# Last block of a decoder: expert tiles' results stored by ScalarE, and dense pairs' exponentials issued two segments behind their scores

## The chip, the cores and the metric

The kernel runs on one core of a Trainium2 chip. The metric is the time of one execution on the device in microseconds (us). The core has five engines with an instruction queue each: TensorE (PE; its weight loads are shown as PEld), VectorE (DVE), ScalarE (ACT), GpSimd (POOL) and SyncE (SP). SyncE computes nothing; it issues DMA transfers. Other engines can issue transfers too, and an engine that issues one spends time of its own queue on it. An engine works through its queue in order; semaphores make it wait for the others.

## The reference

The program is a decoder of six sub-blocks on `x` of 16 samples x 256 positions x 256 features, f32, each with a LayerNorm ahead and a residual add behind. The change lies in the last one, in which each of 8 heads picks one of 8 experts for its values and one for its output:

```
q = (x @ w_q) -> 8 heads of 64;   k = (x @ w_k) -> 8 heads of 64
gates = sigmoid(x @ w_gate)                     # position, head, expert
gm = one_hot(argmax(gates)) * gates             # one expert per position and head
values = einsum('bhne,ehdk,bnd->bhnk', gm, value_experts, x)
attn = softmax(causal(q / 8 @ k.T))
out = attn @ values
out = einsum('bhne,ehkd,bhnk->bhnd', gm, output_experts, out)
x = x + out.sum(heads)
```

## The kernel before, in words

**Two ways through the output experts.** A *pair* is two heads of one sample; there are 4 pairs a sample. The first 13 samples (52 pairs) go the *sparse* way, the last 3 samples (12 pairs) the *dense* way.

In the sparse way the attention outputs of a pair, already scaled by gate and softmax sum, are scattered by GpSimd's indirect DMAs (L1673) into DRAM arrays `zd`, one for each head, in which the rows stand sorted by expert. Then 136 *units* work on these rows. A unit is 2 tiles of 128 rows of one head. `load2` (L1709) has SyncE load it from `zd` into one of six buffers, up to six units ahead of its use; `transposed2` transposes both tiles on TensorE into a PSUM buffer `ps_z2` (L1718) and ScalarE copies that to `zT` (L1720); `expert5` multiplies each tile by its expert's weights on TensorE into `po_t` (L1736), ScalarE copies the result to `y` (L1741, three buffers in turn), and a 256 KB transfer takes `y` to a DRAM array `yd` (L1742). Units of two neighbouring heads alternate, and up to two later units are transposed ahead of a unit's products. When all 34 units of a pair of heads are through, GpSimd gathers rows of `yd` back to the samples' order by indirect DMA (L1685), and VectorE adds them to `x` (L1692).

In the dense way a pair's outputs go through all eight output experts: the gates are broadcast to 64 partitions by two 512 KB loads on SyncE (L1836, `w<-gd`), VectorE multiplies the attention output by each, and 32 products on TensorE add up in one PSUM buffer `po` (L1865) over the four pairs of a sample.

**The order of the work** is written out by hand: inside this block the program keeps the order of the code on TensorE, VectorE, GpSimd and ScalarE. A loop over steps `s` does one sparse pair at a time in a pipeline of stages (`step5`), with `spot5` between the stages: a spot puts in at most one unit, further additions, and gathers that can start. From step 52 on, each step also starts a dense pair (`pair5`, a generator). A `yield` ends a *segment* of a pair. At each step, `advance` runs one segment of each live pair, ordered by a key that the pair itself gave: 0 attention products and the multiplications by the gates (of the pair started four steps ago), 1 scores (one step ago), 2 transposes of the second head (three steps ago), 3 queries and keys (this step), 5 output products (five steps ago), 6 preparations for a later sample, 9 scaling by the softmax sums, gate loads, gated values and transposes of the first head (two steps ago). After each segment `between` runs; from step 52 on it puts in two spots.

**The scores segment** (`causal_pair`, L244 to L264): TensorE writes the scores of the pair into `sc`, of which there is one buffer (L244); VectorE adds the causal mask (L249) and takes the row maxima (L259); the exponentials (L264, one for each half of the rows and each head, four in all) are ScalarE's. For dense pairs they are handed back as a function and put into the list `deferred`, which is worked off when all segments of the step are through, so behind the transposes' copies (`head_T`, L290) of the segment with key 9. The next user of `sc` is the next step's scores segment.

All other products of the block share one PSUM pool `mm` of four buffers, taken in turn: `ps_qk` (queries and keys, copied by ScalarE, L1510 and L1511), `ps_ve` (gated values, read by VectorE, L1525), the heads' transposes `tr` (L289; copied to `pT` by ScalarE, L290), `av`, `ps_z2` and `po_t`.

Of the 136 stores of units, 68 are issued from 3057 to 3297 us of the profiled span, 34 from 3321 to 3455 and 34 from 3549 to 3652; the dense steps start at about 3510.

Of the kernel before, what the change touches and what calls it, by code (L numbers as in the profile page):

```python
# [27 lines left out]
def decoder(ctx: ExitStack, tc: tile.TileContext, a: dict, out: bass.AP):  # L28
# [3 lines left out]
    nc = tc.nc  # L32
# [1420 lines left out]
    with ExitStack() as st:  # L1453
# [36 lines left out]
        def mm5(shape, name):  # L1490
            return psum.tile(shape, F32, tag="mm", name=name, bufs=4)
# [4 lines left out]
        def takes(us):  # L1496
            clock["pe"] += us
# [4 lines left out]
        def queries_keys(b, hp):  # L1502
            takes(1.7)
            hT = hTs5[b]
            cols = slice(hp * P, (hp + 1) * P)
            ps = mm5([P, 2, S], "ps_qk")
            for i in range(2):
                two_k(ps[:, i, :], lambda c: wfqk[i][:, c, cols], lambda c: hT[:, c, :])
            qk = pool.tile([P, 2, S], F32, tag="qk", name="qk", bufs=2)
            nc.scalar.mul(qk[:, 0, :], ps[:, 0, :], 0.125)  # L1510
            nc.scalar.copy(qk[:, 1, :], ps[:, 1, :])  # L1511
            return qk

        def gated_values(b, hp, vv, t):

            takes(3.4)
            tv = pool.tile([P, 2, 8, 64], F32, tag="tv", name="tv", bufs=1)
            for j in range(2):
                ps = mm5([P, 8, 64], "ps_ve")
                two_k(  # L1520
                    ps.rearrange("p e k -> p (e k)"),
                    lambda c: hTs5[b][:, c, t * P : (t + 1) * P],
                    lambda c: wve[hp][:, j, c, :],
                )
                nc.vector.tensor_tensor(  # L1525
                    tv[:, j], ps,
                    gms5[b][:, t, 2 * hp + j, :].unsqueeze(2).to_broadcast([P, 8, 64]), ALU.mult,
                )
            nc.vector.tensor_tensor(tv[:, :, 0:4, :], tv[:, :, 0:4, :], tv[:, :, 4:8, :], ALU.add)
            nc.vector.tensor_tensor(tv[:, :, 0:2, :], tv[:, :, 0:2, :], tv[:, :, 2:4, :], ALU.add)  # L1530
            nc.vector.tensor_tensor(vv[:, t], tv[:, :, 0, :], tv[:, :, 1, :], ALU.add)
# [199 lines left out]
        def expert5(u, at):  # L1731
            q, j, g = UNITS[u]
            zT = zT2s.pop(u)
            po = mm5([P, 2, D], "po_t")
            for i in range(2):
                nc.tensor.matmul(  # L1736
                    po[:, i, :], lhsT=zT[:, i, :],
                    rhs=w_oe[:, bass.ds(at[i] + 2048 * q, D)], start=True, stop=True,
                )
            y = pool.tile([P, 2, D], F32, tag="y5", name="y5", bufs=3)  # L1740
            nc.scalar.copy(y, po)  # L1741
            nc.sync.dma_start(  # L1742
                out=yds[2 * q + j][2 * P * g : 2 * P * (g + 1), :]
                .rearrange("(i p) d -> p i d", p=P),
                in_=y,
            )
# [73 lines left out]
        def pair5(b, hp):  # L1820
            gm = gms5[b]
            n = 4 * b + hp
            qk = queries_keys(b, hp)
            yield 1
            takes(0.9)
            (pr, sm), exps = causal_pair(pool, psum, qk, bufs=1, keep=2, small=4)
            deferred.append(exps)
            yield 9
            nc.vector.reciprocal(sm, sm)
            for qt, sl, w in ((0, slice(0, P), P), (1, slice(P, 384), S)):  # L1830
                for j in range(2):
                    nc.scalar.mul(pr[:, j, sl], pr[:, j, sl], sm[:, qt, j : j + 1])
            gr = grs[n % 2]
            for j in range(2):
                h = 2 * hp + j
                nc.sync.dma_start(  # L1836
                    out=gr[64 * j : 64 * j + 64].rearrange("p e s -> p (e s)"),
                    in_=gds5[b][8 * h : 8 * h + 8, :]
                    .rearrange("e s -> (e s)")
                    .partition_broadcast(64),  # L1840
                )
            vv = pool.tile([P, 2, 2, 64], F32, tag="vv", name="vv", bufs=2)
            for t in range(2):
                gated_values(b, hp, vv, t)
                spot5(step_at[0])
            pT = pool.tile([P, 2, 384], F32, tag="pT", name="pT", bufs=2)
            for j in range(2):
                head_T(pr, pT, j)
                yield 2 if j == 0 else 0
            takes(0.9)  # L1850
            av = mm5([P, S], "av")
            causal_pair_av(av, lambda t, j: vv[:, t, j, :], pT)
            ut = uts[(n + 1) % 2]
            for g in range(2):
                es = slice(4 * g, 4 * g + 4)
                nc.vector.tensor_tensor(
                    ut[:, es, :], gr[:, es, :], av.unsqueeze(1).to_broadcast([P, 4, S]), ALU.mult
                )
            yield 5
            if hp == 0:  # L1860
                pos[b] = psum.tile([P, 2, 512], F32, tag="po", name="po", bufs=1)
            po = pos[b][:, :, 0:D]
            for t in range(2):
                for e in range(8):
                    nc.tensor.matmul(  # L1865
                        po[:, t, :], lhsT=ut[:, e, t * P : (t + 1) * P], rhs=woe[hp][:, e, :],
                        start=(hp == 0 and e == 0), stop=(hp == 3 and e == 7),
                    )
                takes(3.5)
                if t == 0:  # L1870
                    spot5(step_at[0])
            if hp == 3:
                nc.vector.tensor_tensor(xs[b], xs[b], po, ALU.add)  # L1873
                nc.sync.dma_start(out=out[b].rearrange("(t p) d -> p t d", p=P), in_=xs[b])
# [26 lines left out]
        deferred = []  # L1901
# [5 lines left out]
        def new_before(b):  # L1907
            return (6, before5(b, mm5))

        with tc.manual_schedule(engines={mybir.EngineType.PE, mybir.EngineType.Pool, mybir.EngineType.DVE,  # L1910
                                         mybir.EngineType.Activation}):
            s = 0
            while s < END or live or gath or gathering:
                more = []
                step_at[0] = s
                if s < NSB:
                    def gates(b=s):
                        ohs5[b] = gates5(b, mm5, gms5[b], gval[:, 2 * b : 2 * b + 2, :]
                                         .rearrange("p t h -> p (t h)"))
                    more.append(gates)  # L1920
                if 0 <= s - 1 < NSB:
                    more.append(lambda: ranks5(s - 1))
                if s + 2 < NSB and s >= 0:
                    more.append(lambda: rows5(s + 2, mm5, h5[0]))
                for b, q in scat.get(s + 1, ()):
                    if q == 0:
                        back5(b)
                sc = list(scat.get(s, ()))
                for b, q in sc:
                    scatter5(b, q, 0, False)  # L1930

                def second(sc=sc):
                    for b, q in sc:
                        scatter5(b, q, 1, True)
                loads5(s)
                if s < NS + 3:
                    more.append(second)
                    step5(s, more)
                else:
                    second()  # L1940
                if s + 3 < NSB:
                    h5 = [normed(5, s + 3)]
                if s >= NSB:
                    next(plan, None)
                if s == NS - 4:
                    advance(live, [new_before(NSB)])
                elif live or NS <= s < END:
                    new = []
                    if NS <= s < END:
                        b, q = DENSE[s - NS]  # L1950
                        new.append((3, pair5(b, q)))
                        if q == 2 and b + 1 < NB:
                            new.append(new_before(b + 1))

                    def between():
                        if s >= NS:
                            spot5(s)
                            spot5(s)

                    advance(live, new, between)  # L1960
                    while deferred:
                        deferred.pop(0)()
                if s >= END:
                    for _ in range(4):
                        takes(2.0)
                        spot5(s)
                s += 1
# [74 lines left out]
```

## Time and profile before

| | |
|---|---|
| median of 3 runs | 3822.43 us (3819.25 to 3825.97) |
| profiled execution | 3819.31 us; its span 3817.5 us |
| mean granted clock of TensorE | 0.98 |
| TensorE busy | 3588.7 us (94%) |
| VectorE busy | 2290.7 us (60%) |
| ScalarE busy | 1732.0 us (45%) |
| GpSimd busy | 1352.8 us (35%) |
| last block with units, 3100 to 3660 us: TensorE idle | 20.7 + 28.5 + 25.1 us |
| the rest, 3660 to 3817 us: TensorE idle | 11.8 us |

The profile is of one execution; its span runs from the first instruction to the last, and the time of the execution has 1.8 us more. The idle rows come from the busy time by stretch (3100 to 3300, 3300 to 3510, 3510 to 3660, 3660 to 3817). In the groups and timelines, `L244` is line 244 of the kernel, `out<-in` are the program's names for what an instruction writes and reads, and a bracket such as `[2.44 <-ACT pr L264]` gives the engine's idle time just before the instruction and what ended it. `ACTq` and `SPq` are the queues of transfers that ScalarE and SyncE issue.

### The profile page before, as it was taken

The numbers are of one execution on the slowest core, as the hardware profiler recorded it, in microseconds if no ns is written. First come the engines' busy times: TensorE is split into PE (matmuls) and PEld (weight loads), VectorE is DVE, ScalarE is ACT, GpSimd is POOL, SyncE is SP. The second block draws the span as 40 slices with busy tenths as digits, with TensorE's granted clock in tenths as the row PEclk, the third lists the DMA queues.
The fourth block names the chain that finished last, engine by engine and source line by source line (L and its number), as shares of the span: only waits on it lengthen the run. The fifth ranks groups of instructions, "written<-read, shape, count | busy, mean of one in ns | idle before, by whom it ended". The sixth has DMA issues, their size and how long they took to land. (4 is left out here: it accounts for less than half of the span.)

```text
span 3817.5 us, 66392 instructions
## 1 busy us (share of the span) xinstructions
PE 3588.7 (94%) x23024; PEld 2585.0 (68%) x23024; DVE 2290.7 (60%) x6518; ACT 1732.0 (45%) x5178; POOL 1352.8 (35%) x1764
## 2 busy tenths in 40 slices
PE   8999999999999999969999889999999998888899
PEld 6777776777777777759987666665655565555566
DVE  6666667655555565542226776777897643546465
ACT  4555554555555555524435555665322243332431
POOL 3333332233433343342224553222005523545441
PEclk9999999999999999979999999999999999999999
DMA  8000000010000000032234100000000033343553
GB/s 291 1 1 1 1 1 1 1 59 10 17 18 15 12 18 15 15 89 73 71 111 166 29 23 19 29 29 7 8 18 29 25 117 118 110 128 86 165 154 88
DMA packets 190823, 207.16 MB, mean 54 GB/s; under 512 B 56944, under 2 KB 159800, under 8 KB 188960
## 3 DMA queue, kind: packets, MB, share of 16 engines
q1 hardware_dynamic: 160288, 142.68, 12.2%
q0 software_dynamic: 25168, 51.85, 4.8%
q10 hardware_dynamic: 5040, 8.40, 0.7%
q8 instruction: 189, 3.10, 0.4%
q14 instruction: 138, 1.13, 0.1%
HBM read 122.93 MB, written 79.92 MB: 53 GB/s over the span
## 5 line engine op out<-in xcount | busy, mean ns | idle before, releaser
L289 PEld LDWEIGHTS tr<-ident,pr 128*128 128x128 f32 x2176 | 276.3, 142 | 160.7 <-issue 89.7
L201 PE MATMUL ps_ve<-w_ve,w 128*128 128x512 f32 x768 | 364.8, 619 | 11.2 <-DVE tv L1525 3.3
L289 PE MATMUL tr<-ident,pr 128*128 128x128 f32 x2176 | 346.4, 275 | 25.4 <-ACT zT L528 10.4
L483 POOL TENSOR_TENSOR pr<-pr,sm 128x512 f32<-128x512 f32 x256 | 264.4, 1055 | 282.3 <-DVE sm L481 142.0
L279 POOL TENSOR_TENSOR pr<-pr,sm 128x256 f32<-128x256 f32 (+1 forms) x256 | 206.5, 828 | 424.0 <-DVE sm L277 313.4
L477 ACT ACTIVATE pr<-sc,nmx 128x256 f32<-128x256 f32 x512 | 237.1, 472 | 251.1 <-DVE nmx L472 174.0
L1673 POOL DMA_INDIRECT zd<-zu,slots x208 | 208.0, 1000 | 395.8 <-DVE slots L1595 187.1
L273 ACT ACTIVATE pr<-sc,nmx 128x128 f32<-128x128 f32 (+1 forms) x512 | 209.8, 418 | 266.8 <-DVE nmx L271 225.7
L1685 POOL DMA_INDIRECT g<-yo,slots x208 | 205.2, 987 | 267.8 <-DVE x L1692 188.9
L472 DVE CUSTOM_DVE_ANT_0 sc<-sc,mk 128x256 f32<-128x256 f32 x512 | 211.2, 444 | 112.1 <-PE sc L462 59.4
L1525 DVE TENSOR_TENSOR tv<-ps_ve,gms 128x512 f32<-128x512 f32 x208 | 140.6, 688 | 216.0 <-PE ps_ve L201 161.7
L201 PE MATMUL ps_qk<-hT,w_a 128*128 128x256 f32 x1024 | 258.8, 386 | 0.0
L201 PEld LDWEIGHTS ps_ve<-w_ve,w 128*128 128x128 f32 x768 | 145.2, 199 | 165.7 <-issue 141.2
L290 DVE COPY pT<-tr 128x384 f32<-128x384 f32 (+1 forms) x384 | 223.2, 594 | 18.9 <-PE tr L289 12.8
L290 ACT COPY pT<-tr 128x512 f32<-128x512 f32 (+1 forms) x256 | 137.5, 538 | 148.7 <-PE tr L289 130.0
L201 PEld LDWEIGHTS ps_qk<-hT,w_a 128*128 128x128 f32 x1024 | 179.8, 190 | 29.1 <-issue 11.8
L244 PE MATMUL sc<-qk 64*128 64x128 f32 (+1 forms) x1536 | 162.2, 343 | 17.5 <-ACT pr L264 15.8
L249 DVE TENSOR_TENSOR sc<-sc,cneg 128x512 f32<-128x512 f32 x192 | 133.1, 693 | 73.2 <-remote 32.5
L1736 PE MATMUL po_t<-w_oe,zT 128*128 x544 | 149.5, 400 | 29.2 <-ACT zT L1720 20.5
L1346 DVE TENSOR_REDUCE nm<-sc 128x4 f32<-128x1024 f32 x128 | 150.7, 1221 | 33.4 <-PE sc L1340 33.4
L271 DVE TENSOR_REDUCE nmx<-sc 128x2 f32<-128x256 f32 (+1 forms) x256 | 136.8, 555 | 49.4 <-ACT pr L273 46.9
L902 DVE COPY wt<-m_w 128x1024 f32 x71 | 49.3, 694 | 186.0 <-PE ps_h L201 184.2
(334 smaller groups left out, 8236.3 us busy)
## 6 DMA issues: line engine op xcount, KB each, us to landing
yo<-y SPq DMA_DIRECT2D x136, 256.0 KB
w<-gd SPq DMA_DIRECT2D x24, 512.0 KB
yd<-y SPq DMA_DIRECT2D x71, 128.0 KB
zd<-zero SPq DMA_DIRECT2D x8, 1088.0 KB
z<-zd SPq DMA_DIRECT2D x136, 64.0 KB
c<-in_ctxT SPq DMA_DIRECT2D x32, 256.0 KB
m_w<-in_m_w SPq DMA_DIRECT2D x16, 512.0 KB
x<-in_x SPq DMA_DIRECT2D x16, 256.0 KB
```

Of the source, the lines that this page charges most:

```text
L201: nc.tensor.matmul(ps, lhsT=lhsT(c), rhs=rhs(c), start=(c == 0), stop=(c == 1))
L244: nc.tensor.matmul(sc[:, j, at : at + ks], lhsT=qk[rows, 0, qs], rhs=qk[rows, 1, 0:ks], start=True, stop=True,)
L273: nc.scalar.activation(pr[:, j, sl], sc[:, j, sl], AF.Exp, bias=nmx[:, qt, j : j + 1], accum_out=sm[:, qt, j : j + 1],)
L279: nc.gpsimd.tensor_tensor(pr[:, :, sl], pr[:, :, sl], sm[:, qt, :].unsqueeze(2).to_broadcast([P, 2, n]), ALU.mult,)
L289: nc.tensor.transpose(tr[:, at : at + P], src, ident)
L290: copy(pT, tr[:, 0 : P * len(blocks)])
L472: nc.vector.tensor_tensor_reduce(out=sc[:, j, t, :], in0=sc[:, j, t, :], in1=mk[:, t, :], scale=-1.0, scalar=3.4e38, op0=ALU.add, op1=ALU. ...
L477: nc.scalar.activation(pr[:, j, t, :], sc[:, j, t, :], AF.Exp, bias=nmx[:, j, t : t + 1], scale=-1.0, accum_out=sm[:, j, t : t + 1],)
L483: nc.gpsimd.tensor_tensor(pr[:, j], pr[:, j], sm[:, j, :].unsqueeze(2).to_broadcast([P, 2, S]), ALU.mult)
L1346: last4[0] = nc.vector.tensor_reduce(nm[:, :, c0 : c0 + 33 : 32], scs[i].rearrange("p j t k -> p t j k"), AX.X, ALU.max, negate=True,)
L1673: nc.gpsimd.indirect_dma_start(out=zds[h], out_offset=bass.IndirectOffsetOnAxis(ap=slots5[:, 2 * b + t, h : h + 1], axis=0), in_=zr[:, t, ...
L1685: nc.gpsimd.indirect_dma_start(out=g, out_offset=None, in_=yds[h], in_offset=bass.IndirectOffsetOnAxis(ap=slots5[:, 2 * b + t, h : h + 1], ...
```

## The change

There are two parts. The store of a unit's result `y` to DRAM is issued by ScalarE, directly behind ScalarE's copy that makes `y`, where SyncE issued it. And the exponentials of a dense pair no longer wait for the end of the step: each entry of `deferred` carries a count of 2, `between` lowers it after every segment, and runs the exponentials when it is 0. The first lowering comes directly after the scores segment itself, the second after the segment behind it, and there the exponentials stand ahead of the spots. What is left at the end of a step is run there, as before.

```
             y = pool.tile([P, 2, D], F32, tag="y5", name="y5", bufs=3)
             nc.scalar.copy(y, po)
-            nc.sync.dma_start(
+            nc.scalar.dma_start(
                 out=yds[2 * q + j][2 * P * g : 2 * P * (g + 1), :]
                 .rearrange("(i p) d -> p i d", p=P),
                 in_=y,
...
             (pr, sm), exps = causal_pair(pool, psum, qk, bufs=1, keep=2, small=4)
-            deferred.append(exps)
+            deferred.append([2, exps])
             yield 9
...
                     def between():
+                        for x in deferred:
+                            x[0] -= 1
+                        while deferred and deferred[0][0] == 0:
+                            deferred.pop(0)[1]()
                         if s >= NS:
                             spot5(s)
                             spot5(s)
 
                     advance(live, new, between)
                     while deferred:
-                        deferred.pop(0)()
+                        deferred.pop(0)[1]()
```

More of the change, by code (lines that the diff above doesn't have):

```diff
@@ L1741, in expert5 @@
             nc.scalar.copy(y, po)
-            nc.sync.dma_start(
+            nc.scalar.dma_start(
                 out=yds[2 * q + j][2 * P * g : 2 * P * (g + 1), :]
@@ L1826, in pair5 @@
             (pr, sm), exps = causal_pair(pool, psum, qk, bufs=1, keep=2, small=4)
-            deferred.append(exps)
+            deferred.append([2, exps])
             yield 9
@@ L1955, in between @@
                     def between():
+                        for x in deferred:
+                            x[0] -= 1
+                        while deferred and deferred[0][0] == 0:
+                            deferred.pop(0)[1]()
                         if s >= NS:
@@ L1961, in decoder @@
                     while deferred:
-                        deferred.pop(0)()
+                        deferred.pop(0)[1]()
                 if s >= END:
```

## The prediction

> **What bounds the kernel now.** I read the busy line of the page first, then the last block in stretches, then TensorE's waits there, and last the chain of work that ended last. Busy time of the whole span, and of two stretches of the last block (PE, PEld, DVE, ACT, POOL busy us with counts; granted clock; DMA share; GB/s):
>
> ```profile
> PE 3588.7 (94%) x23024; PEld 2585.0 (68%) x23024; DVE 2290.7 (60%) x6518; ACT 1732.0 (45%) x5178; POOL 1352.8 (35%) x1764
> 3510.00:3660.00 150.00, 124.90 (x541) 81.25 (x539) 73.60 (x158) 55.97 (x157) 61.85 (x63) 0.97 0.51 145
> 3660.00:3817.00 157.00, 145.17 (x639) 102.01 (x639) 94.18 (x180) 32.28 (x109) 45.74 (x48) 1.00 0.43 115
> ```
>
> TensorE is the bound: 94% of the span. What a change is worth here is the TensorE idle time that it removes or adds; 25.1 us of it lie in 3510 to 3660, and 11.8 us in 3660 to 3817. What ended TensorE's waits, first in 3510 to 3660 (two lines), then in 3660 to 3817 (us in total, times, longest):
>
> ```profile
> PE sc L244 <- ACT pr L264: 4.6, 2, 2.4
> PE ps_z L1718 <- ACT pr L264: 2.0, 2, 1.0
> ```
>
> ```profile
> PE sc L244 <- ACT pr L264: 8.3, 6, 1.4
> ```
>
> So of the last 11.8 us, 8.3 are one wait: a dense pair's scores (L244) wait for the exponentials (L264) of the pair before, because both use the one PSUM buffer `sc`. The chain shows the same in each of the last steps:
>
> ```profile
> 3691.51 6.87 PE ps_ve L201 x16
> 3699.22 1.63 ACT pr L264 x8
> 3700.90 0.93 PE sc L244 x8
> ```
>
> ScalarE's exponentials are the only link of this tail that is not TensorE's.
>
> **Order.** In the built programs the order on TensorE, VectorE and GpSimd is the same before and after; only ScalarE's and SyncE's orders change. So everything comes through those two queues.
>
> **Part 1: exponentials earlier.** Before, they follow the whole step, behind the copy of the last transposes (the first head's, `head_T` 0), and the next step's scores are 1.0 us of products away. After, they follow the segment next to the scores: in a full step, the second head's copy (`head_T` 1). The next scores are then a step (some 19 us) away, and the wait goes. The six waits of the tail are 1.39 us each (8.3 us). The other two:
>
> ```profile
> 3519.67 0.93 PE L244 MATMUL sc<-qk 64*128 64x128 f32 x8 [2.44 <-ACT pr L264]
> 3533.44 0.93 PE L244 MATMUL sc<-qk 64*128 64x128 f32 x8 [2.19 <-ACT pr L264]
> ```
>
> The first waits for the first dense pair, whose step has only scores and one projection: its exponentials stay where they are, so 2.44 us stay. The second goes: 2.19. Together 8.3 + 2.2 = 10.5 us off the path.
>
> What becomes late instead: ScalarE now asks for the maxima (L259) soon after the scores. VectorE reaches them late in the tail:
>
> ```profile
> 3684.64 0.39 ACT L1510 ACTIVATE qk<-ps_qk 128x256 f32<-128x256 f32 x1 [1.25 <-issue]
> 3685.89 0.69 DVE L249 TENSOR_TENSOR sc<-sc,cneg 128x512 f32<-128x512 f32 x1
> 3686.61 1.02 DVE L259 TENSOR_REDUCE nmx<-sc 128x2 f32<-128x256 f32 x2
> ```
>
> So ScalarE waits at the exponentials until 3687.6, takes about 2 us, and the copies of `qk` (L1510, L1511) behind them end near 3690.5 instead of 3685.3. Their users are the next scores (3700.9) and the fourth `ps_ve` group of the step, which takes the same PSUM buffer (the pool has four; the group starts 5.2 us after 3691.35). Cover is 6 us, cost 0; were it gone, a step would lose up to the 5 us of delay. Second, TensorE comes 1.4 us earlier to the transposes of the second head, whose PSUM buffer VectorE must have emptied (L1525). In the trace that ended at 3680.4 against a new start of 3680.95, so 0.3 us are left after a semaphore's way, and 0.8 us a step later. I put 0.5 us for all six; bounds 0 and 3 x 1.39 = 4.2, as VectorE is crowded in the three steps with many gather additions only.
>
> In 3546 to 3653, where tiles run between segments, the block of exponentials moves from ahead of one pair of tiles to ahead of another. The 2.0 us at `ps_z` go there, and something like half returns at the new place: -1.0, bounds -2 and +2.
>
> **Part 2: stores on ScalarE.** 136 stores leave SyncE (0.36 us of issue each) and go behind their copies. The price of that pattern is in this trace, in an earlier block, where ScalarE stores its own copies (L318, L319):
>
> ```profile
> 2009.86 0.59 ACT L318 COPY k<-ps_k 128x512 f32<-128x512 f32 x1 [1.14 <-PE ps_k L201]
> 2010.47 0.33 ACTq L319 DMA_DIRECT2D kd<-k  x1
> 2010.84 0.80 ACT L1091 COPY at<-sc 128x768 f32<-128x768 f32 x1 [0.40 <-PE sc L1079]
> ```
>
> From copy to next instruction: 0.98 us. Without a store the next starts 0.48 us after such a copy starts (L1741 at 3615.21, L1720 at 3615.69; pipelined copies overlap by 0.1). So 0.50 us each, 136 x 0.50 = 68 us of ScalarE, which is busy 37% (56.0 of 150 us) where it is fullest. How much reaches TensorE? Queued behind a store are the next tile's transposed copy (L1720), its result copy (L1741), and `pT`, `qk` or exponentials. I went through the 20 TensorE waits between 3050 and 3660 that ScalarE ended (40.5 us): a result copy lies within 0.5 us ahead of the releasing instruction in three, so 3 x 0.5 = 1.5 us. New waits of that kind, where slack was under 0.5 us: I take as many again, 1.5. Bounds: 0, and 34 x 0.5 = 17 us if every store between 3549 and 3652 counts. I stay near the low end, since 102 of 136 stores stand in stretches with one tile at a time.
>
> What SyncE gains: its loads `z<-zd` no longer stand behind stores that wait for copies.
>
> ```profile
> SPq L1742 <- ACT y L1741: 114.7, 74, 6.8
> ```
>
> ```profile
> ACT y L1741 <- DMA yo<-y: 1.2, 3, 0.6
> ```
>
> The 114.7 us are SyncE's and no TensorE wait in the last block was ended by such a load (they run six tiles ahead), so 0. The second line (from 3546 to 3655) is what ScalarE lost to stores landing late: 1.2 us at most, taken as 0. GpSimd's queue is not touched; its gathers wait for the stores' landing, once 17.1 us, and that is hidden. The stores take turns on the eight completion semaphores with SyncE's DMAs, so 36 of them also wait for the DMA eight places back; in the times of before, that had always landed by then, by 2 us or more: 0, and up to 4 us each on a broadcast load (`w<-gd`) if one is late.
>
> [...]
>
> **Sum.** -10.5 + 0.5 - 1.0 + 1.5 + 1.5 = -8.0 us. The profiled execution took 3819.31 us (span 3817.5), so 3811.3 for it; it lies 3.1 us under the median of the three runs, 3822.43, and against that the sum is 3814.4. I forecast 3814.4.
>
> **Rivals.**
> - ScalarE sets the pace of the tiles (slower). Between the tiles of 3546 to 3653 ScalarE's share of a tile rises from 0.76 to 1.26 us, TensorE's is about 1.3; after 2 us of exponentials the backlog hardly drains. For: TensorE already waits for L1720 and L1741 there. Against: ScalarE idles 63% of that stretch. It decides when more than 36 stores reach TensorE in full: 36 x 0.5 = 18 us, the 10.5 of the gain and 7.6 beyond. Price: 34 x 0.5 + 102 x 0.1 = 27 us, less 10.5: 3839. Chance 0.15. [...]
> - No gain in the tail: TensorE, freed from the exponentials, waits for VectorE's L1525 at the next transposes instead. For: 0.3 us of slack in the step at 3680. Against: the later steps have more, and the last three few additions. Price: the 8.3 shrink to 2, so 3820.7. Chance 0.15.
> - Stores free more than they cost: the idle time before L1741 that the trace calls remote (9.8 us from 3546 to 3655) was partly late buffers, and SyncE's freed queue ends it: 3814.4 - 3 - 8 = 3803. Against: TensorE's own end came late in the same places. Chance 0.15.
> - That the change does nothing is excluded: ScalarE's order differs in nearly every full dense step.
>
> **How the numbers follow.** My forecast has 0.55, with its own range 3809 to 3820. About 0.2%, 7.6 us, is what a measurement of this kernel can tell from no change: that line is 3814.8, and my forecast sits on it. Of the 0.55 I put 0.37 under it and 0.18 above. Faster: 0.37 + 0.15 = 0.52; within: 0.18 + 0.15 = 0.33; slower: 0.15. The range reaches a little past the fast rival's 3803, to 3801, and, above, past the no-gain rival with the new waits at 6 us: 3826.
>
> **What would show it.** After: the row `sc` L244 waiting for `pr` L264 falls from 8 times to one or two (2.4 us); ScalarE's exponentials wait some 4 us for L259 in each tail step; ScalarE's queue shows 136 stores of 0.33 us; the tail from the last tile to the end is 8 us shorter. Wrong it would be if TensorE's waits at `ps_z`, `po_t` or `tr` grow by over 3 us in 3050 to 3650, or if a wait for L1525 takes the place of the exponentials.

## The result, and the profile after

| | before | after |
|---|---|---|
| median of 20 runs, us | 3822.39 (3816.11 to 3832.19) | 3814.63 (3804.11 to 3826.91) |
| ratio | | 0.9979, 95% interval 0.9971 to 0.9988 |
| span of the profiled execution, us | 3817.5 | 3813.8 |

That is 0.21% faster, 3814.63 us against the forecast of 3814.4. The number is right; whether the reasons are is for the experiments, since the sum had terms of opposite sign.

The busy line of the page after, and the same two stretches (columns as before):

```profile
PE 3596.1 (94%) x23024; PEld 2589.9 (68%) x23024; DVE 2291.3 (60%) x6518; ACT 1736.6 (46%) x5178; POOL 1355.0 (36%) x1764
```

```profile
3510.00:3660.00 150.00, 126.30 (x533) 82.46 (x533) 70.53 (x151) 57.79 (x161) 63.94 (x65) 0.94 0.53 147
3660.00:3817.00 157.00, 147.31 (x639) 103.13 (x639) 94.29 (x180) 31.32 (x103) 46.90 (x48) 0.98 0.43 115
```

In the last stretch TensorE is busy 2.1 us longer for the same 639 matmuls: its granted clock is 0.98 where it was 1.00, and in the stretch ahead of it 0.94 where it was 0.97. TensorE's waits after, first in 3510 to 3660 (some lines), then in 3660 to the end:

```profile
PE ps_z L1718 <- ACT y L1741: 2.9, 3, 1.2
PE sc L244 <- ACT pr L264: 2.4, 1, 2.4
PE ps_z L1718 <- DMA z<-zd: 2.4, 2, 1.4
```

```profile
PE ps_qk L201 <- issue: 1.6, 1, 1.6
PE tr L289 <- DVE tv L1525: 0.3, 1, 0.3
```

The wait at `sc` fell from eight times to the one that the prediction left in place, and in its stead TensorE waits 0.3 us, once, for VectorE's L1525 (the 1.6 us ahead of `ps_qk` are laid to no wait). ScalarE waits in the tail as described, and the copies of `qk` come late. The second line names no releaser for its 5.80 us; in the quieter traces below six such waits are laid to the maxima (L259), 30.2 us in all with the exponentials alone:

```profile
3680.16 0.48 ACT L290 COPY pT<-tr 128x384 f32<-128x384 f32 x1 [1.66 <-PE tr L289]
3686.44 0.37 ACT L264 ACTIVATE pr<-sc,nmx 128x128 f32<-128x128 f32 x1 [5.80 <-issue]
...
3688.04 0.39 ACT L1510 ACTIVATE qk<-ps_qk 128x256 f32<-128x256 f32 x1
```

The line that the prediction put at nothing, ScalarE waiting for a store to land before it may write the next `y`, is larger (same stretch as before, 3546 to 3655):

```profile
ACT y L1741 <- DMA yo<-y: 4.8, 5, 1.9
```

**Where this pair of traces fails.** The order on TensorE is the same in both, so the same instructions can be compared. Cut at the first tile's transposes, at the first dense pair's scores and at the seventh's (start of the first of the eight matmuls of L244), the stretches are:

| us | to the first tile | first tile to first dense scores | first to seventh dense scores | from there to the last matmul |
|---|---|---|---|---|
| before | 3054.6 | 458.5 | 148.1 | 151.8 |
| after | 3057.6 | 452.0 | 150.3 | 149.4 |

The tail gives 2.4 us and not 8. TensorE was busy 2.1 us longer in it, at the lower clock (0.98 against 1.00); the other 3.5 us are laid to nothing here. And the largest difference, 6.4 us, lies where only the stores changed. In both traces that stretch is full of stalls of 3 to 5 us. One trace of each cannot tell the terms apart; the parts had to be run alone.

### The profile page after: what moved, and what is told of

Same layout as the page of the kernel before. It is cut to its first block, busy times and chain, and to the rows that moved or that the text cites. A ratio compares the mean times of both kernels' runs of the same rounds, so it can differ in the third digit from the quotient of the medians.

```text
span 3813.8 us, 66165 instructions
## 1 busy us (share of the span) xinstructions
PE 3596.1 (94%) x23024; PEld 2589.9 (68%) x23024; DVE 2291.3 (60%) x6518; ACT 1736.6 (46%) x5178; POOL 1355.0 (36%) x1764
## 4 chain that ended last, share of the span: by engine, by line
PE 80%; DVE 12%; issue 3%; ACT 2%; another core or an unknown queue 1%; DMA 1%; POOL 1%; ACTq 0%; DVEq 0%; SPq 0%; POOLq 0%
PE ps_qk L201 14%; PE ps_ve L201 11%; PE ps_v L201 7%; PE po L534 6%; PE tr L289 5%; PE sc L244 4%; PE ps_h L201 3%; PE po L926 3%; PE po_t L1736 3%; PE sc L462 2%; PE av L519 2%; PE po L1865 2%; PE sc L1340 2%; PE sc L1366 2%; PE av L295 2%
## 5 line engine op out<-in xcount | busy, mean ns | idle before, releaser
L289 PE MATMUL tr<-ident,pr 128*128 128x128 f32 x2176 | 346.1, 275 | 24.6 <-ACT zT L528 10.5
L1525 DVE TENSOR_TENSOR tv<-ps_ve,gms 128x512 f32<-128x512 f32 x208 | 140.6, 688 | 211.5 <-PE ps_ve L201 160.9
L290 DVE COPY pT<-tr 128x384 f32<-128x384 f32 (+1 forms) x384 | 223.3, 595 | 19.8 <-PE tr L289 12.6
L201 PEld LDWEIGHTS ps_qk<-hT,w_a 128*128 128x128 f32 x1024 | 179.9, 190 | 29.1 <-issue 11.8
L244 PE MATMUL sc<-qk 64*128 64x128 f32 (+1 forms) x1536 | 163.1, 345 | 7.0 <-ACT pr L264 5.3
L902 DVE COPY wt<-m_w 128x1024 f32 x71 | 49.3, 694 | 188.0 <-PE ps_h L201 186.3
```

The lines of the kernel that those rows point to most:

```text
L201: nc.tensor.matmul(ps, lhsT=lhsT(c), rhs=rhs(c), start=(c == 0), stop=(c == 1))
L244: nc.tensor.matmul(sc[:, j, at : at + ks], lhsT=qk[rows, 0, qs], rhs=qk[rows, 1, 0:ks], start=True, stop=True,)
L289: nc.tensor.transpose(tr[:, at : at + P], src, ident)
L290: copy(pT, tr[:, 0 : P * len(blocks)])
```

## The experiments

All experiments ran beside the kernel before, which took 3712 to 3715 us in these sessions (it was 3822 in the first comparison). There were three sessions, each on another chip: first the two parts, the doubled stores and the three segments; then the whole change and the two halves of the stores; then the four runs on the broadcast loads. Differences in us below are the ratio's, times 3713. Where two runs of one session are compared, their medians are given too, since the two measures can disagree by some us. The traces of these sessions are far quieter: from the first tile to the first dense scores the kernel before takes 387.7 us with 7.0 us of idle TensorE, where the first trace had 458.5 with 49.3. So here the stretches can be compared.

### The two parts alone

Stores only (the exponentials stay at the end of the step):

```
-            nc.sync.dma_start(
+            nc.scalar.dma_start(
                 out=yds[2 * q + j][2 * P * g : 2 * P * (g + 1), :]
```

> Only the stores of y move to ScalarE; the exponentials stay at the end of the step as in the kernel before. Theory A (the recorded one: the exponentials give -11.0 us, the stores cost +3.0): about 3 us slower than before, 0 to 17, and the six waits of 1.39 us at sc stay in the tail. Rival B (ScalarE sets the pace of the tiles): 17 to 27 us slower. Rival C (the freed SyncE queue helps: part of the 7.8 us that the change gave comes from the stores): 3 to 8 us faster than before.

Measured: ratio 1.0016 (1.0007 to 1.0025), 5.9 us slower.

Exponentials only:

```
-            deferred.append(exps)
+            deferred.append([2, exps])
...
+                        for x in deferred:
+                            x[0] -= 1
+                        while deferred and deferred[0][0] == 0:
+                            deferred.pop(0)[1]()
```

> Only the exponentials move; SyncE keeps the stores. Theory A: 11 us faster than before, so some 3 us faster than the changed kernel, with one wait of 2.4 us left at sc. Rival B: as much as 20 us or more faster than the changed kernel's stores allow, so the same 11 us here. Rival C: 0 to 5 us faster than before, since the stores gave the rest.

Measured: ratio 0.9975 (0.9965 to 0.9985), 9.3 us faster.

The whole change, in a later session with the two halves of the stores:

> The changed kernel once more, beside the kernel before and the two halves of its stores, on one chip. From the parts measured apart (exponentials alone 9.4 us faster, stores alone 5.7 us slower): 3 to 5 us faster than before if they add up; 8 us, as in the first comparison, if the stores cost less once the exponentials are out of their way.

Measured: ratio 0.9989 (0.998 to 0.9998), 4.1 us faster. The parts add up: -9.3 + 5.9 = -3.4. By these figures half of what the exponentials bring is lost to the stores. Theory A has the signs right; its 3.0 us for the stores is half of the 5.9 measured, and still inside the interval (2.6 to 9.3). Rival B (17 us and more) and rival C (the stores help) fall.

The kernel before was also profiled here:

> The kernel before itself, for a trace on this chip: the time within 0.2% of its other runs here, and in the trace six waits of 1.39 us at sc in the tail.

Measured: 3714.4 us, and the six waits. TensorE's waits in the tail of the kernel before, and then with the exponentials alone:

```profile
PE sc L244 <- ACT pr L264: 8.3, 6, 1.4
```

```profile
PE tr L289 <- DVE tv L1525: 0.4, 1, 0.4
```

This is the tail of the prediction: 8.3 us go, and 0.4 us are left at VectorE's L1525. The stretches, cut at the same instructions as above, with TensorE's idle time and the rest (which grows when the clock is low: further down, the same four products take 2.08 us at a granted clock of 0.50 and 1.03 us at 1.00):

| us (idle, rest) | first tile to first dense scores | first to seventh dense scores | from there to the last matmul |
|---|---|---|---|
| before | 387.7 (7.0, 380.6) | 140.5 (19.3, 121.2) | 151.7 (6.9, 144.8) |
| stores only | 387.7 (7.1, 380.6) | 145.6 (22.1, 123.5) | 151.7 (6.9, 144.8) |
| exponentials only | 387.7 (7.0, 380.6) | 135.0 (15.3, 119.8) | 145.7 (0.6, 145.1) |
| both | 387.9 (7.2, 380.6) | 144.1 (20.0, 124.1) | 144.6 (0.0, 144.6) |

The 102 stores of the first stretch cost nothing that can be seen; what the stores cost lies in the second stretch, where units run between dense segments, and in these traces about half of it is not idle time: 2.3 of 5.1 us for the stores only against the kernel before, and 4.3 of 9.1 us for both against the exponentials alone. The granted clock, in stretches of 10 us from 3450 to 3580, is under 1.00 in four with both parts (0.93, 0.90, 0.84 and 0.81) and in two with the exponentials alone (0.96 and 0.87), so there most of it is the lower clock: 10.2 us at 0.50 against 3.4, so some 3.4 us of the 4.3 (an estimate from these times). With the stores only and in the kernel before it is 0.83 in one stretch each, and what the 2.3 us are was not shown.

### Which stores

```
+            store = nc.scalar if q < 3 else nc.sync      # the other run: q == 3
-            nc.scalar.dma_start(
+            store.dma_start(
```

> Exponentials moved; ScalarE stores only the first 102 units (the stretches with sparse pairs), SyncE the last 34 (between the dense segments). Theory A (only where units come in a row does a store stand in TensorE's way): the same as exponentials alone within 1.5 us, 9 us faster than before. Rival (every store costs 6/136 us, wherever it stands): 4.3 us above exponentials alone, 5 us faster than before.

Measured: ratio 0.9976 (0.9966 to 0.9986), 8.9 us faster.

> Exponentials moved; ScalarE stores only the last 34 units, SyncE the first 102. Theory A: the whole cost of the stores, 5 to 6 us, is here, so 3 to 5 us faster than before, and the stretch from the first dense scores to the sixth pair's is about 140 us against 135 in the run with the exponentials alone. Rival: 1.5 us above exponentials alone, 8 us faster than before.

Measured: ratio 0.9983 (0.9974 to 0.9992), 6.3 us faster; second stretch 137.8 us.

The first 102 stores are free (8.9 against 9.3). The last 34 cost 3.0 by the ratios against the exponentials alone, and 4.3 by the medians of these two runs, which share a session (3706.77 and 3702.44); the 6.3 us lie outside both forecasts (3 to 5, and 8). In the second stretch this run issues its stores just as the whole change does, and yet its trace has 137.8 us (18.2 idle, 119.6 the rest) where the other has 144.1 (20.0, 124.1). So the place of the cost is shown. Its size is not: two executions that issue the stores of this stretch alike differ there by more than the 5.2 us between both parts and the exponentials alone.

### ScalarE's time or something else

Each store as two, so that ScalarE issues twice as often:

```
-            nc.scalar.dma_start(
-                out=yds[2 * q + j][2 * P * g : 2 * P * (g + 1), :]
-                .rearrange("(i p) d -> p i d", p=P),
-                in_=y,
-            )
+            for i in range(2):
+                nc.scalar.dma_start(
+                    out=yds[2 * q + j][P * (2 * g + i) : P * (2 * g + i + 1), :], in_=y[:, i, :],
+                )
```

> The changed kernel with each store of 256 KB issued as two of 128 KB, both by ScalarE: 136 more issues of 0.33 us and the gaps around them, some 0.37 us, so 50 us more of ScalarE. Theory A: the cost on the path follows ScalarE's time, 3.0 x 0.37 / 0.50 = 2.2 us above the changed kernel, so 5 to 6 us under before. Rival B: 10 us or more above the changed kernel. Rival C: ScalarE's time is off the path and the time is the changed kernel's within 1 us.

Measured: ratio 1.0004 (0.9995 to 1.0013), 1.5 us slower than before, so 5.6 above the changed kernel. Between theory A (2.2) and rival B (10), and not rival C. Of it 2.4 us are in the first stretch (390.3 us) and 1.6 in the tail (146.1), and not only where the stores had cost before, so it isn't simply the same cost doubled; the run also makes twice as many transfers.

Then the traces. ScalarE's waits for stores, from 3445 to 3562 us, in the kernel before, with the exponentials alone, and with both:

```profile
ACT y L1741 <- DMA yo<-y: 9.1, 7, 2.6
```

```profile
ACT y L1741 <- DMA yo<-y: 5.8, 4, 2.3
```

```profile
ACT y L1741 <- DMA yo<-y: 11.0, 6, 4.3
```

There are three `y` buffers, and a copy waits until the store three units back has landed. SyncE's queue shows what stands ahead of the late stores. In the kernel before (start, us from the first to the last of a group, count at the end):

```profile
3455.44 0.42 SPq L1709 DMA_DIRECT2D z<-zd  x1
3456.34 0.45 SPq L1836 DMA_DIRECT2D w<-gd  x1
3456.89 2.22 SPq L1742 DMA_DIRECT2D yo<-y  x2
3459.19 1.03 SPq L1709 DMA_DIRECT2D z<-zd  x2
3460.55 0.36 SPq L1742 DMA_DIRECT2D yo<-y  x1
3460.97 0.47 SPq L1836 DMA_DIRECT2D w<-gd  x1
```

With both parts of the change:

```profile
3454.32 0.45 SPq L1836 DMA_DIRECT2D w<-gd  x1
3454.86 1.69 SPq L1709 DMA_DIRECT2D z<-zd  x2
3456.60 0.71 SPq L1836 DMA_DIRECT2D w<-gd  x1
3458.82 24.64 SPq L1709 DMA_DIRECT2D z<-zd  x9
```

Before, three stores, each of which has to wait for its copy, stood between the two 512 KB loads of a pair, and the second started 4.6 us behind the first. Now it starts 2.3 us behind the first, and at the next pair 1.1 us (3485.54 to 3486.68), where it was 5.5. At the third and last pair among the stores it is 0.5 us, and it was some 1.7 already in the kernel before and with the exponentials alone. From the records of the packets, counted from the start of the issue, the stores issued behind the first of these pairs land after 6.0, 7.7, 5.8 and 6.1 us (issued 3455.59 to 3463.12); the stores of the same four units took 3.7, 4.4, 5.1 and 5.7 us in the kernel before. Over all 34 stores the mean hardly differs: 3.7 us, against 3.5 to 3.7 in the kernel before and 3.2 to 3.4 with the exponentials alone, where other transfers of SyncE's queue blur the count. So it is a few stores that come late, and not all. What a late store does to TensorE, with both parts (ScalarE, then TensorE):

```profile
3532.49 0.37 ACT L1720 COPY zT<-ps_z 128x256 f32<-128x256 f32 x1 [0.44 <-ACT y L1741]
3537.17 0.58 ACT L1741 COPY y<-po_t 128x512 f32<-128x512 f32 x1 [4.31 <-DMA yo<-y]
```

```profile
3533.67 1.03 PE L1736 MATMUL po_t<-w_oe,zT 128*128 x4
3537.81 0.69 PE L1718 MATMUL ps_z<-ident,z 128*128 128x128 f32 x2 [3.11 <-ACT y L1741]
3538.90 2.08 PE L1736 MATMUL po_t<-w_oe,zT 128*128 x4 [0.40 <-ACT qk L1511]
```

ScalarE stands 4.31 us, TensorE 3.11 us; and behind that the same four products take 2.08 us where they took 1.03. The clock of that stretch with both parts (columns as in the prediction's first fence; clock third from the end):

```profile
3530.00:3540.00 10.00, 5.93 (x25) 4.44 (x26) 2.44 (x7) 4.42 (x15) 0.00 (x0) 0.84 0.78 207
3540.00:3550.00 10.00, 10.00 (x40) 8.46 (x39) 0.00 (x0) 1.54 (x3) 0.00 (x0) 0.81 0.23 80
```

So here the wait is paid for twice: the 3.11 us as they stand, and 1.05 us more for the four products behind it, at the lower clock. In this trace the granted clock is 0.50 from 3468.6 to 3472.0 us and from 3536.9 to 3543.7, and 1.00 in between; 10.2 us at half the clock are some 5 us of work (an estimate from these times). The first drop stands behind a wait of 1.97 us (to 3468.23), and the second sets in 2.2 us after the last product ahead of the 3.11 us. That the waits bring the drops on is inferred from where they stand; no run shows it by itself.

Not every such wait has a lower clock behind it. In the trace with only the last 34 stores on ScalarE, ScalarE waited 3.55 us for a store at the same place and TensorE up to 2.2 us, and the clock stayed at 1.00 in the same two stretches:

```profile
3530.00:3540.00 10.00, 7.16 (x35) 5.78 (x34) 2.01 (x6) 2.94 (x8) 0.00 (x0) 1.00 0.59 194
3540.00:3550.00 10.00, 10.00 (x39) 6.84 (x38) 1.63 (x3) 3.14 (x7) 1.91 (x2) 1.00 0.20 67
```

Most of the 6.3 us between the two traces is in the rest, 4.5 us (124.1 against 119.6), and the estimate from the clock above is some 5. The eleven runs of the whole change spread over 12.6 us, with a mean granted clock of 0.988 in the fastest and 0.986 in the slowest.

That gave a new theory, D: a collision of stores and broadcast loads, which without the stores start closer together. Its rival, S, is ScalarE's own time. First the loads were left out, with the stores on ScalarE and on SyncE:

```
-            for j in range(2):
-                h = 2 * hp + j
-                nc.sync.dma_start(
-                    out=gr[64 * j : 64 * j + 64].rearrange("p e s -> p (e s)"),
...
```

> The changed kernel without the 24 broadcast loads of the gates (w<-gd); the dense pairs multiply by whatever lies in that buffer, so their three samples' outputs are not the reference's. To be read against the next run. Theory D (the stores' cost in the last 34 units is a collision: with SyncE free of the stores, the two 512 KB loads of a pair start closer together, the results' stores behind them land in 6 to 8 us, and the copies wait for one of the three y buffers): without these loads the copies' wait for stores falls from 11 us to under 4 us, and the time is that of the next run within 1.5 us. Theory S (each store costs by its own time in ScalarE's queue): 4 to 6 us above the next run.

> The run with the exponentials alone (stores on SyncE), without the 24 broadcast loads, so its three dense samples' outputs are not the reference's either. Theory D: 0 to 3 us faster than exponentials alone (9.4 us under before), so 9 to 12 us under before, and as fast as the run above. Theory S: 4 to 6 us under the run above.

Measured: 0.9959 (0.9946 to 0.9973) and 0.9955 (0.9942 to 0.9969), 15.2 and 16.7 us faster than before. In medians 3699.40 us (3698.95 to 3702.86) and 3698.25 us (3697.61 to 3699.87): 1.2 us between stores on ScalarE and on SyncE (1.5 by the ratios), where with the loads it is 5.2. ScalarE's waits for stores are gone from both traces. So the 4 to 6 us of theory S don't show: without the loads, the place of the stores hardly matters. In the two traces the second stretch still differs by 3.0 us (134.5 against 131.5), so up to that is ScalarE's own. Two things limit this. The 4 us by which the two differences differ are no more than the intervals allow. And theory D expected the second run 9 to 12 us under before, and it is 16.7: without the loads the stores on SyncE gain 7.4 us too. So the loads cost that version as well. The share of the 16 DMA engines bears this out: from 3460 to 3470 us it is 1.04 in the kernel before, 1.03 with the exponentials alone and 1.01 with both, so full in all three, and 0.83 and 0.85 without the loads. These two runs, which take away 24 transfers of 512 KB, tie the cost to the loads; they don't show that it hangs on how close together the loads start.

Then the loads were kept and spaced: the second load of a pair is queued on SyncE behind an earlier tile load, so that five to six tile loads lie between two broadcast loads.

```
-            nc.sync.dma_start(
+            z_load.append(nc.sync.dma_start(
                 out=z2s[u % 6][:, :, 64 * j : 64 * j + 64],
...
+            gates_load(0)
             vv = pool.tile([P, 2, 2, 64], F32, tag="vv", name="vv", bufs=2)
             for t in range(2):
                 gated_values(b, hp, vv, t)
                 spot5(step_at[0])
+            with tc.issue_after(z_load[-6].ins):
+                gates_load(1)
```

> The changed kernel with the second broadcast load of each pair queued on SyncE behind the sixth-last tile load traced so far, so that five to six tile loads lie between two broadcast loads where one or two did. Theory D: the stores land sooner, and 3 to 6 us of the stores' cost are won: 6 to 9 us faster than before. Theory S: as the changed kernel, 3.3 us faster than before, within 2 us.

Measured: 0.9983 (0.9974 to 0.9992), 6.3 us faster, at the lower end of theory D's 6 to 9 and above theory S. Against the changed kernel it is 2.2 us better by the ratios, less than the 3 to 6 us that theory D expected (5.4 by the medians, each against the kernel before of its session), and the intervals overlap. ScalarE's waits for stores fall from 11.0 to 7.1 us and the second stretch from 144.1 to 138.4, which is no more than the two executions above differed by; the mean landing stays at 3.8 us. The edit reached two of the three pairs: their loads start 9.4 and 11.8 us apart, but those of the third still 0.5 us, and behind it stands the longest wait for a store (3.80 us).

> Exponentials moved, stores on SyncE, broadcast loads spaced as in the run above. Theory D: there the stores already space the loads, so within 2 us of exponentials alone, 9.4 us faster than before; a little faster if the waits for stores (5.8 us in that trace) shrink further. Theory S: the same.

Measured: 0.997 (0.9958 to 0.9982), 11.1 us faster; with the exponentials alone it was 9.3 and the intervals overlap, as expected. With the same spacing, stores on SyncE are 4.8 us better than stores on ScalarE by the ratios, but 1.6 by the medians (3705.01 and 3706.56), the intervals overlap, and ScalarE waits for stores equally long in both traces (7.1 us). So how much of the collision is the closeness of the two loads stays open. Two other ways were not taken apart. In the kernel before, loads of any kind stand in SyncE's queue behind stores that wait for their copies (18.8 us of such waits from 3415 to 3560). And with the stores on ScalarE, SyncE's transfers wait for stores to land: 20.2 us from 3415 to 3562 with both parts (10.3 at L1709 and 9.9 at L1836), and never there in the kernel before or with the exponentials alone.

### How far behind the scores

```
-            deferred.append([2, exps])
+            deferred.append([3, exps])
```

> The changed kernel with the exponentials three segments behind the scores, behind the copies of qk, where it has two. ScalarE no longer waits for the maxima (L259) ahead of the copies of qk. Theory A: that wait is covered, so the same time as the changed kernel within 2 us, and the six waits at sc stay away, since the next scores are still more than 10 us off. Rival (the late copies of qk do cost TensorE, some 1 us a step): 3 to 6 us under the changed kernel.

Measured: 0.9997 (0.9988 to 1.0006), 1.1 us faster than before, so 3.0 us worse than the changed kernel by the ratios, where at most 2 were expected; the intervals overlap, and the second stretch is alike (144.4 against 144.1 us). The rival falls: late copies of `qk` cost nothing that this won back. Whether three segments are worse than two stays open.

## Why the prediction was right or wrong

- **The time and the sign**: right in the first comparison (3814.63 against 3814.4; 0.21% faster). In the later session the same pair is 4.1 us apart (0.7 to 7.4), under the 8.0 of the sum and within 0.2%. The intervals of the two sessions overlap; if the change gave more in the first, that is not explained here.
- **Exponentials, -10.5 + 0.5 - 1.0 = -11.0**: measured -9.3 (-13.0 to -5.6). The six tail waits went as forecast (8.3 us to 0.4), the first wait of 2.4 us stayed, the 2.19 us wait went, and the maxima's new wait on ScalarE (5.80 us in the line shown) was covered. The 0.5 us for VectorE's L1525 shows as 0.3 to 0.4 us. The -1.0 at `ps_z` can't be told apart: its waits for the exponentials went (1.1 us to none), and those for the copies L1741 and L1720 grew (1.9 us to 8.1).
- **Stores, +1.5 + 1.5 = +3.0**: measured +5.9 (2.6 to 9.3) alone, 5.2 beside the exponentials, 3.0 with the last 34 only. The price of one store was about right (0.37 us of issue against 0.33, and 1.02 us from a copy's start to the next instruction, 3522.83 to 3523.85, against 0.98), and so was the place (the last 34, the first 102 free). The times alone don't rule out the size. The way was another: the sum has only ScalarE's own time at the stores, and without the broadcast loads moving them costs 1.2 to 1.5 us (up to 3.0 in the traces). The waits for stores to land and the lower clock are not in it.
- **The step that failed** is the one on what SyncE gains: "so 0", and its second line, "1.2 us at most, taken as 0". The 114.7 us that SyncE spent waiting at stores were read as idle time of an engine off the path. They also held back the loads behind the stores and kept the broadcast loads of two pairs apart (4.9 and 5.5 us with the exponentials alone, 2.3 and 1.1 with both). With the stores gone from SyncE, ScalarE's wait for stores grew from 1.2 to 4.8 us in the first pair of traces and from 5.8 to 11.0 between exponentials alone and both, TensorE stood up to 3.11 us, and its granted clock was 0.50 for 10.2 us from 3450 to 3580, where with the exponentials alone it was for 3.4. Without the broadcast loads, 1.2 to 1.5 of the 5.2 us are left. That the broadcast loads are part of the cost is shown; whether by their closeness, by loads of any kind that come forward, or by the completion semaphores that stores and loads share (the same eight in the traces before and after; in the one after, 36 of ScalarE's 136 stores have a wait on a semaphore ahead of them), stays open. The bound given for the last, up to 4 us for each store that waits for a broadcast load, may have been touched once: with both parts, a copy of `pT` behind a store stood 2.0 us until a broadcast load landed. That was not tried by itself.
- **The rivals**: that ScalarE sets the pace of the tiles fell (5.9 us for the stores, not 27), and so did the idea that freed buffers help: that rival saw the right place, the `y` buffers, with the wrong sign. The rival of no gain in the tail fell with the 0.4 us at L1525.
- **The total came out because** the first session's difference was 8 us; the sum of the parts as measured is -3.4, and in the first pair of traces the tail gave 2.4 us where some 8 were forecast, and the stretch that only the stores could touch gave 6.4. That the forecast lies 0.2 us from the first result is luck.

## What to carry to other kernels

A queue that waits can also be a brake: here SyncE's waits at the stores kept two broadcast loads 4.6 us apart that started 2.3 us apart without them. Before moving transfers to another engine, list which transfers stood behind them and will now start earlier, and what they will run into. Count buffers against landing time, not only against the issue cost: with three buffers and four stores issued in 7.5 us (3455.59 to 3463.12), stores that took 5.8 to 7.7 us to land left ScalarE waiting, 3.13 us the longest there. The version to keep here is the exponentials moved and the stores left on SyncE: 9.3 us faster than before, and 5.2 us faster than the changed kernel by the ratios, though these two intervals overlap.

## What the runs showed of the hardware that was not expected

The kernel before took 3822 us in the first comparison and 3712 to 3715 us in the later sessions. 71 of the 109 us are in the stretch from the first tile to the first dense scores (458.5 against 387.7 us; clock 0.93 in 3060 to 3500 us against 1.00 in 3060 to 3410), in stalls like the first of these lines, of the first trace from 3060 to 3510, which has no counterpart in the other session's trace:

```profile
PE po_t L1736 <- ACT zT L1720: 20.5, 5, 5.1
PE po_t L1736 <- issue: 5.0, 2, 2.8
```

Their cause was not found. A difference of a few us in such a stretch says nothing on a change, however well it fits.

From 3400 us on, the granted clock in these traces is 1.00 or 0.50, and 0.50 comes in pieces of 3.4 or 6.8 us (with both parts from 3468.6 to 3472.0 and from 3536.9 to 3543.7; with the exponentials alone from 3489.2 to 3492.6). The piece at the very end of each trace is left out. What brings one on was not shown: a wait of 1.97 us was followed by one, and a wait of 2.19 us, with the last 34 stores on ScalarE, was not. Each 3.4 us at half the clock are 1.7 us of work, by estimate.
